# A layer of RWKV attention and mixture of experts: eight settings of its instruction planner, and the issuing engine of the last transfer

## The chip, the cores and the metric

The kernel runs on one core of a Trainium2 chip. Time is device time in microseconds (us), and the number that counts is the median over runs of the kernel: 462.02 us from 3 runs (461.55 to 462.97). The engines are called PE (TensorE, matrix products), PEld (its weight loads), DVE (VectorE), ACT (ScalarE), POOL (GpSimd) and SP (SyncE, which issues most transfers).

## What is computed

The input x has 2 x 2048 tokens of 256 channels in f32. It is normalized, and from the normalized xn two branches are computed and added to x:

```python
x = L0_attn_x                       # (2, 2048, 256)
xn = _layernorm(x, axis=-1)
x = x + attention(xn) + moe(xn)

# attention: v, r = xn @ value_w.T, sigmoid(xn @ recep_w.T)
# a scan over time with the state (aa, bb, pp):
#   wkv_t = (e1 * aa + e2 * v_t) / (e1 * bb + e2 + 1e-6)
#   aa = e1b * aa + e2b * v_t ;  bb = e1b * bb + e2b
# out = (r * wkv) @ out_w.T

# moe: scores = softmax(xn @ gate_w.T + gate_b), the best 2 of 8 experts
# each expert: (silu(xn @ w1.T + b1) * (xn @ w3.T + b3)) @ w2.T + b2
# a shared expert of the same form, hidden size 512, for every token
```

## The kernel before, in words

**Tiles.** The 4096 tokens are 8 chunks of 512. `ORDER` is 2, 3, 0, 1, 4 (called `FIRST`) and 5, 6, 7 (called `LAST`). A time step s of the attention covers the chunks 2s and 2s + 1, one for each batch row.

**Stages.** Each chunk is loaded, normalized, transposed by PE (L579) and copied out of PSUM (L593). Router scores are made (by_e L602, by_t L612, sc L615). When all eight chunks are scored, VectorE does the routing (L651 to L768, with two small counting products on PE, cp L690 and L691): each token is given two slots among 66 tiles of 128 rows. POOL then scatters the normalized rows to those slots in DRAM (xs_d, L795, 64 transfers). The tiles follow in the order `SEQ`: 25 double tiles of 256 rows for one expert (`double_flow`, ph L1357, silu L1343, product L1370, pos L1380, bias L1387), and single or mixed tiles (`tile_flow`, L1255 to L1307). POOL scatters their results to ys_d (L1319). When the last tile is stored, `collect_flow` loads the two results of every token (y, L1400), VectorE adds them with their weights to the chunk's sum (`combine_flow`, L1410), and the chunk goes to the output in halves (`out_flow`, L1446), the very last one in quarters.

Beside this runs the dense work. The shared expert has four pieces of 128 hidden channels for each chunk (`hidden_flow`: p L1003, silu L1009, gated product L1023 on VectorE, or L1016 and L1019 on ACT and POOL for pieces that are planned while the routing runs). The attention has, for each of 4 time steps and 2 halves of the channels, a chain on VectorE and ACT (`attention_flow`, L872 to L921) and for each batch row a flow with the products v and r (`mix_flow`, L935; uu L945, scan L950, rw L957, th L963, L967 to L977). `dense_flow` multiplies hidden pieces and attention with their output weights (po L1086) and adds them to the chunk's sum (L1102; L1112 for the closing quarters). A chunk's sum begins as x plus a bias (L1046). The sums of `FIRST` chunks go to DRAM (part_d) in between and are taken up again; those of `LAST` chunks begin only at the end.

**What sets the order.** Nothing is scheduled at run time: every engine goes through its instructions in the order in which the program lists them. A planner (class `Plan`) writes that list. Each piece of work is a generator, a flow, that asks for an engine and a duration in ns (`on(690, "DVE")`), for rooms (buffers such as the 8 PSUM banks `PS` or the 32 general buffers `U`), and may wait for events. The planner takes the request that can start first by its own durations. Among those that can start within 150 ns of it on the same engine it takes the one with the lowest rank. `plan.add(flow, rank)` gives a flow's rank, and `rank=` in a single request overrides it. `spare=(PS, n)` says that n banks must be left free. Ranks that matter here: routing 0.5, transposes 1.0 to 1.7, collecting 3, tiles 10, the projections v and r 9, the attention chain 20, the mix flows 20 to 23, L1023 15, dense work of `FIRST` 25 to 34, hidden pieces 30 and more, dense sums of `LAST` 45 to 47, combines 45.

**Settings that the change touches:**

- `BETWEEN` (used where the hidden flows are added, at the end of the function): for these chunks of the order the first hidden piece gets the rank of the transposes instead of 30 and more.
- `EAGER`: the attention begins when this chunk of the order is transposed.
- `AHEAD`: hidden pieces of the first `LAST` chunk (chunk 5) that may be made before the tiles and are kept in their U buffers until the end.
- all other pieces of `LAST` chunks wait for the event `turn` of a tile near the end of `SEQ` (its first products have been listed).
- `SOON`: how many tiles ahead `goes_flow` loads the row numbers of a group of eight tiles (meta L1233, then L1237 and L1238), which the scatters to ys_d need.

Of the kernel before, what the change touches and what calls it, by code (L numbers as in the profile page):

```python
# [51 lines left out]
NT = W // P  # L52
# [124 lines left out]
def on(ns, engine, *take, table=None, spare=None, rank=None):  # L177
    return ({engine: ns}, table, take, spare, rank)
# [14 lines left out]
NT = W // P  # L193
# [12 lines left out]
DBL = 2 * (PAIRS // (2 * P) - (E - 1))  # L206
# [6 lines left out]
SEQ = sorted(PLACE, key=PLACE.get)  # L213
assert sorted(SEQ) == [*range(0, DBL, 2), *range(DBL, TILES)]
AT = {j: n for n, j in enumerate(SEQ)}
# [24 lines left out]

LATE = 3000

BETWEEN = (1, 3)

EAGER = 6
MORE = 8

QUICK = 2
# [4 lines left out]

WARM = 10

SOON = 8

BACK = 5

AHEAD = [(LAST[0], i) for i in range(3)]  # L260

LEFT, RIGHT = ORDER[:4], ORDER[4:]

# [2 lines left out]
def rwkv_moe_kernel(  # L266
# [55 lines left out]
    def rows(t, c):  # L322
        return t[c % B, ts(c // B, W), :].rearrange("(n p) c -> p n c", p=P)
# [460 lines left out]
    def scatter_flow():  # L784


        yield have["routed"]
        yield 600
        for side, chunks in (("left", LEFT), ("right", RIGHT)):
            for c in chunks:  # L790
                for n in range(NT):
                    g = c * NT + n
                    for w in range(2):
                        yield on(1410, "POOL")
                        step = nc.gpsimd.indirect_dma_start(  # L795
                            out=xs_views[2 * g + w],
                            out_offset=bass.IndirectOffsetOnAxis(ap=slot[w][:, g : g + 1], axis=0),
                            in_=xn[c][:, n, :],
                            in_offset=None,
                        )  # L800
                        if w:
                            keep_pace(step)
                land(0, [scattered[c]])
            early[side].__exit__(None, None, None)
            if side == "left":
                pool = ctx.enter_context(tc.tile_pool(name="bias", bufs=1, side="left"))
                late["b2"] = pool.tile([P, E, C], F32, tag="b2", name="b2")
                late["still"] = ctx.enter_context(tc.tile_pool(name="still", bufs=3, side="left"))
                late["rows"] = ctx.enter_context(tc.tile_pool(name="late_rows", bufs=2, side="left"))
                late["bcol"] = ctx.enter_context(tc.tile_pool(name="bcol", bufs=3, side="left"))  # L810
                plan.add(bias_flow(), 0)
            else:
                late["pool3"] = ctx.enter_context(tc.tile_pool(name="late3", bufs=2, side="right"))
                late["ys"] = ctx.enter_context(tc.tile_pool(name="late_ys", bufs=3, side="right"))
                late["h"] = ctx.enter_context(tc.tile_pool(name="late_h", bufs=3, side="right"))
        yield LATE
        for j in SEQ:
            plan.add((double_flow if j < DBL else tile_flow)(j), 10 + AT[j] / 100)
        for j in TOGETHER:
            plan.add(rows_flow(j), 10 + AT[j] / 100)  # L820
            flow = still_flow if j < DBL else one_flow if j < UNI else quarters_flow
            plan.add(flow(j), (9 if j < DBL else 15) + AT[j] / 100)
        for j in range(0, TILES, GO):
            plan.add(goes_flow(j), 10 + needed(j) / 100)
        plan.add(collect_flow(), 3)
# [99 lines left out]
    def mix_flow(s, ch, b, e1b, e2b, e1, e2, ready, of_state, of_v, left):  # L925
        c = B * s + b
        of = f"{c}_{ch}"
        yield turned[c]
        yield have["wa"]
        yield ready  # L930

        def project(name):
            pt = bank([P, W], f"{name}p_{of}")
            for k in range(NC):
                nc.tensor.matmul(  # L935
                    pt, wa[name][:, k, ts(ch, P)], xnT[c][k], start=(k == 0), stop=(k == NC - 1)
                )
            xnT_used(c)
            return pt

        yield on(1722, "PE", (PS, 1), spare=(PS, 2), rank=9)
        v = project("wv")
        yield on(690, "DVE", single("uu"))
        uu = wide("uu", of)
        nc.vector.tensor_tensor(uu, e2b, v, ALU.mult)  # L945
        yield on(1400, "DVE", single("aa"))
        aa = wide("aa", of, W + 1)
        state = st_aa[:, b, ch : ch + 1]
        nc.vector.tensor_copy(aa[:, 0:1], state)
        nc.vector.tensor_tensor_scan(aa[:, 1:], e1b, uu, aa[:, 0:1], ALU.mult, ALU.add)  # L950
        nc.vector.tensor_copy(state, aa[:, W:])
        single("uu")[0].give()
        yield of_v
        yield on(690, "DVE", (U, 1))
        wkv = u([P, W], f"rw_{of}")
        rw[c, ch] = wkv
        nc.vector.tensor_tensor(wkv, e2, v, ALU.mult)  # L957
        PS.give()
        yield on(1722, "PE", (PS, 1), spare=(PS, 2), rank=9)
        r = project("wr")  # L960
        yield on(600, "ACT", single("th"), table="tanh" if plan.table not in ("exp", "silu") else plan.table)
        th = wide("th", of)
        nc.scalar.activation(th, r, AF.Tanh, scale=0.5)  # L963
        PS.give()
        yield of_state
        yield on(690, "DVE")
        nc.vector.tensor_tensor(aa[:, :W], aa[:, :W], e1, ALU.mult)  # L967
        left[0] -= 1
        if left[0] == 0:
            for name in ("e1", "e2", "e1b", "e2b"):  # L970
                single(name)[0].give()
        yield on(690, "DVE")
        nc.vector.tensor_tensor(wkv, wkv, aa[:, :W], ALU.add)
        single("aa")[0].give()

        yield on(690, "DVE")
        nc.vector.scalar_tensor_tensor(wkv, th, 1.0, wkv, ALU.add, ALU.mult)  # L977
        single("th")[0].give()
        rw_done[c, ch].set()


    def hidden_flow(c, i):

        if (c, i) not in HALVES:
            yield turned[c]
        yield have["ws13", i]
        if c in LAST and (c, i) not in AHEAD:
            yield turn[SEQ[-8]]
        pts = []
        halves = 2 if (c, i) in HALVES else 1  # L990
        for h in range(halves):
            if halves == 2:
                yield half_turned[h]
            of = ts(h, W // halves)
            for m in range(2):
                yield on(
                    1722 // halves, "PE", *([(PS, 2), (U, 1)] if m == h == 0 else []),
                    spare=(U, KEEP if c in FIRST or (c, i) in AHEAD else MORE),
                )
                if h == 0:  # L1000
                    pts.append(bank([P, W], f"p{m}_{c}_{i}"))
                for k in range(NC):
                    nc.tensor.matmul(  # L1003
                        pts[m][:, of], ws13[:, m, k, ts(i, P)], xnT[c][k][:, of], start=(k == 0), stop=(k == NC - 1)
                    )
        xnT_used(c)
        si = u([P, W], f"si_{c}_{i}")
        yield on(690, "ACT", table="silu")
        nc.scalar.activation(si, pts[0], AF.Silu, bias=vec[:, V_BS1 + i : V_BS1 + i + 1])  # L1009
        PS.give()  # L1010
        bs3 = vec[:, V_BS3 + i : V_BS3 + i + 1]
        if have["scores"].at is not None and have["routed"].at is None:

            yield on(690, "ACT", (U, 1))
            t = u([P, W], f"gate_{c}_{i}")
            nc.scalar.activation(t, pts[1], AF.Identity, bias=bs3)  # L1016
            PS.give()
            yield on(1150, "POOL")
            nc.gpsimd.tensor_tensor(si, si, t, ALU.mult)  # L1019
            U.give()  # L1020
        else:
            yield on(750, "DVE", rank=15)
            nc.vector.scalar_tensor_tensor(si, pts[1], bs3, si, ALU.add, ALU.mult)  # L1023
            PS.give()
        hid[c, i] = si
        hid_done[c, i].set()
# [41 lines left out]
    def dense_flow(c, half, shared, attended, ready, done):  # L1068
# [28 lines left out]
        if closes:  # L1097
            return
        yield ready
        yield on(690, "DVE")  # L1100
        both = sums[c][:, 2 * half : 2 * half + 2, :]
        nc.vector.tensor_tensor(both, po, both, ALU.add)  # L1102
        PS.give()
# [225 lines left out]
    def double_flow(j):  # L1329
# [18 lines left out]
        for m in range(2):  # L1348
# [9 lines left out]
                        p[m][:, i, :], mine[k][:, m, ts(i, P)], xT[:, k, :], start=(k == 0), stop=(k == NC - 1)  # L1358
                    )
            if m == 0:  # L1360
                plan.add(silu_flow(), 10 + AT[j] / 100)
        find(AT[j] + 1)
        U.give()
        XST.give()
# [76 lines left out]
    def out_flow(c, first, n):  # L1441

        of = sums[c]
        groups = slice(first, first + n)
        yield on(500, "SP")
        nc.sync.dma_start(rows(out, c)[:, groups, :], of[:, groups, :])  # L1446
        yield 3000
        left[c] += n
        if left[c] == NT:
            X.give()  # L1450
# [21 lines left out]
    plan.add(route_flow(), 0.5)  # L1472
    plan.add(scatter_flow(), 0.5)
    plan.add(bias_rows_flow(), 2)
    plan.add(attention_flow(), 20)

    def then_attend(c):

# [90 lines left out]
```

## Time and profile before

| what | value |
|---|---|
| median of 3 runs | 462.02 us |
| the profiled execution, its own time | 462.66 us |
| its span | 461.0 us |
| mean granted TensorE clock | 0.999 |
| instructions | 6864 |
| moved by DMA | 84.93 MB, mean 184 GB/s |

The span runs from the first to the last instruction; 1.66 us of that execution's time lie around it. A line of a profile names an engine, a line of the kernel, an operation and its output and input tiles. A wait is written as "who <- whom", with its sum, count and longest case in us.

In broad stages the core spends 0 to 40 us on loading, normalizing and transposing, 40 to 66 on the routing, up to about 157 on the scatter (with dense work on PE), 162 to 400 on the tiles, and the rest on results:

```profile
core 0: us, PE busy (x) PEld busy (x) DVE busy (x) ACT busy (x) POOL busy (x), PEclk, DMA share, GB/s
0.00:40.00 40.00, 38.08 (x281) 25.75 (x282) 30.01 (x118) 26.14 (x53) 19.22 (x70) 1.00 1.01 270
40.00:162.00 122.00, 119.57 (x378) 70.77 (x377) 99.61 (x190) 33.46 (x59) 75.18 (x67) 1.00 0.55 164
162.00:400.00 238.00, 236.11 (x1129) 162.00 (x1128) 185.59 (x349) 140.09 (x274) 98.86 (x89) 1.00 0.59 162
400.00:440.00 40.00, 40.00 (x132) 24.70 (x131) 30.98 (x60) 4.75 (x8) 2.19 (x2) 1.00 0.82 276
440.00:461.00 21.00, 15.92 (x73) 13.37 (x71) 15.44 (x31) 0.00 (x0) 0.00 (x0) 0.97 0.63 213
```

The columns are the stretch and its length, then the busy time and the number of instructions of each engine, the granted clock of TensorE, the DMA engines' share and their rate.

### The profile page before, as it was taken

To read this page: it belongs to the slowest core of one execution; us is meant where nothing else is said; L and a number is where in the kernel's file an instruction comes from. 1 tells how busy PE (TensorE), PEld (TensorE's weight loads), DVE (VectorE), ACT (ScalarE), POOL (GpSimd) and SP (SyncE) were. 2 spreads that over 40 slices of the span, in tenths; PEclk is the share of its full clock that TensorE was granted. 3 is DMA by queue.
4 is the path that set the end of the run, shared out by engine and by line. 5 is a ranking of instruction groups with operands and counts; after the bars stand their busy time and mean duration, and the time that the engine had idled before them with its cause. 6 is when DMAs were issued, how large, how long until landed. Compare 5 with 4: busy or idle time off the path is not lost.

```text
span 461.0 us, 6864 instructions
## 1 busy us (share of the span) xinstructions
PE 449.7 (98%) x1985; PEld 296.6 (64%) x1985; DVE 361.6 (78%) x747; ACT 204.4 (44%) x392; POOL 195.5 (42%) x228
## 2 busy tenths in 40 slices
PE   8999899999999989999999999999999999999996
PEld 6664555444787567766767666666765766646875
DVE  6986999968569658997568966986898568788586
ACT  3788210171140219635873569727662763121000
POOL 5730358777777104355434444362536233300000
PEclk9999999999999999999999999999999999999999
DMA  7999942745234697776584697456656330079993
GB/s 234 352 269 189 238 153 80 228 150 183 92 129 148 206 187 213 188 188 176 131 244 122 181 249 211 124 164 166 188 166 213 113 104 25 25 248 302 345 320 126
DMA packets 91508, 84.93 MB, mean 184 GB/s; under 512 B 50445, under 2 KB 76846, under 8 KB 91344
## 3 DMA queue, kind: packets, MB, share of 16 engines
q1 hardware_dynamic: 82672, 61.98, 47.9%
q0 software_dynamic: 7952, 22.23, 15.3%
q10 hardware_dynamic: 848, 0.30, 0.3%
q8 instruction: 16, 0.26, 0.3%
q14 instruction: 20, 0.16, 0.1%
HBM read 44.93 MB, written 26.70 MB: 155 GB/s over the span
## 4 chain that ended last, share of the span: by engine, by line
PE 75%; DVE 11%; DMA 8%; SPq 2%; ACT 1%; issue 1%; DVEq 0%
PE ph L1357 17%; PE p L1003 16%; PE pos L1380 9%; PE po L1086 8%; PE wrp L935 6%; PE wvp L935 5%; PE ph L1255 4%; PE ph L1259 3%; DMA xb<-in_x_dram 2%; DMA out_dram<-pa 2%; PE pos L1297 2%; PE tp L579 2%; PE pos L1301 1%; DVE xb L1410 1%; DMA xn<-in_x_dram 1%; DMA y<-ys_d 1%
## 5 line engine op out<-in xcount | busy, mean ns | idle before, releaser
L1319 POOL DMA_INDIRECT ys_d<-ys,goes x66 | 75.3, 1140 | 142.3 <-DVE ys L1387 63.6
L1003 PE MATMUL p<-xnT,ws 128*128 128x512 f32 (+1 forms) x272 | 115.3, 569 | 1.5 <-DVE rw L957 1.1
L1357 PE MATMUL ph<-xsT,still 128*128 128x256 f32 x400 | 93.0, 380 | 0.0
L1003 PEld LDWEIGHTS p<-xnT,ws 128*128 128x128 f32 x272 | 50.5, 190 | 53.8 <-issue 47.0
L795 POOL DMA_INDIRECT xs_d<-xn,slot x64 | 71.0, 1110 | 30.7 <-issue 14.9
L1357 PEld LDWEIGHTS ph<-xsT,still 128*128 128x128 f32 x400 | 74.8, 190 | 14.1 <-issue 3.9
L1086 PE MATMUL po<-ws,si 128*128 128x256 f32 x256 | 59.4, 380 | 0.5 <-DVE si L1023 0.5
L1086 PEld LDWEIGHTS po<-ws,si 128*128 128x128 f32 x256 | 48.3, 190 | 10.4 <-issue 2.6
L1009 ACT ACTIVATE si<-p,vec 128x512 f32<-128x512 f32 x32 | 21.6, 686 | 74.3 <-PE p L1003 74.2
L1380 PE MATMUL pos<-we,si 128*128 x200 | 48.4, 385 | 1.4 <-DVE si L1370 1.4
L1380 PEld LDWEIGHTS pos<-we,si 128*128 128x128 f32 x200 | 37.0, 190 | 16.6 <-issue 4.3
L1185 ACT COPY own<-we 128x512 f32 x72 | 38.9, 623 | 1.3 <-issue 1.2
L963 ACT ACTIVATE th<-wrp 128x512 f32<-128x512 f32 x16 | 9.5, 596 | 59.2 <-PE wrp L935 59.1
L1343 ACT ACTIVATE si<-ph,bcol 128x256 f32<-128x256 f32 x50 | 21.0, 471 | 29.4 <-PE ph L1357 29.2
L1086 PE MATMUL po<-wo,rw 128*128 128x256 f32 x128 | 31.9, 379 | 0.0
L1387 DVE TENSOR_TENSOR ys<-pos,b 128x512 f32<-128x512 f32 x25 | 17.2, 690 | 17.2 <-PE pos L1380 16.7
L935 PE MATMUL wrp<-xnT,wr 128*128 128x512 f32 x64 | 30.4, 597 | 0.0
L1370 DVE SCALAR_TENSOR_TENSOR si<-ph,bcol,si 128x256 f32<-128x256 f32 x50 | 21.5, 470 | 9.5 <-PE ph L1357 8.8
L935 PE MATMUL wvp<-xnT,wv 128*128 128x512 f32 x64 | 28.8, 592 | 0.0
L1213 DVE STREAM_TRANSPOSE xsT<-xs 128x512 f32<-128x512 f32 (+1 forms) x41 | 24.0, 594 | 5.8 <-DMA xs<-xs_d 5.8
L1023 DVE SCALAR_TENSOR_TENSOR si<-p,vec,si 128x512 f32<-128x512 f32 x29 | 21.4, 743 | 8.6 <-PE p L1003 7.0
L916 DVE RECIPROCAL bb<-bb 128x128 f32<-128x128 f32 x32 | 27.5, 913 | 0.4 <-issue 0.2
(167 smaller groups left out, 614.2 us busy)
## 6 DMA issues: line engine op xcount, KB each, us to landing
still<-we SPq DMA_DIRECT2D x25, 512.0 KB, 3.2
y<-ys_d SPq DMA_DIRECT2D x32, 256.0 KB, 5.3
xs<-xs_d SPq DMA_DIRECT2D x100, 64.0 KB, 2.9
we<-in_w_exp_dram SPq DMA_DIRECT2D x16, 256.0 KB, 11.3
xb<-in_x_dram SPq DMA_DIRECT2D x8, 512.0 KB
pa<-part_d SPq DMA_DIRECT2D x8, 512.0 KB, 5.5
xn<-in_x_dram SPq DMA_DIRECT2D x14, 256.0 KB, 5.2
part_d<-xb SPq DMA_DIRECT2D x5, 512.0 KB, 2.9
```

The costliest lines, as they stand in the source:

```text
L795: step = nc.gpsimd.indirect_dma_start(out=xs_views[2 * g + w], out_offset=bass.IndirectOffsetOnAxis(ap=slot[w][:, g : g + 1], axis=0), in_ ...
L916: nc.vector.reciprocal(den[:, ts(n, P)], den[:, ts(n, P)])
L935: nc.tensor.matmul(pt, wa[name][:, k, ts(ch, P)], xnT[c][k], start=(k == 0), stop=(k == NC - 1))
L1003: nc.tensor.matmul(pts[m][:, of], ws13[:, m, k, ts(i, P)], xnT[c][k][:, of], start=(k == 0), stop=(k == NC - 1))
L1009: nc.scalar.activation(si, pts[0], AF.Silu, bias=vec[:, V_BS1 + i : V_BS1 + i + 1])
L1086: nc.tensor.matmul(po[:, j, :], l[:, ts(2 * half + j, P)], r, start=(i == 0), stop=(i == len(parts) - 1))
L1185: nc.scalar.copy(mine[q, k], we[:, which[j, q], 0:2, k, :])
L1213: nc.vector.transpose(xT.rearrange("p k (b t) -> p b k t", t=Q), t.rearrange("p b (k i) -> p b k i", i=Q))
L1319: nc.gpsimd.indirect_dma_start(out=ys_views[j], out_offset=bass.IndirectOffsetOnAxis(ap=goes[:, j : j + 1], axis=0), in_=y, in_offset=None ...
L1357: nc.tensor.matmul(p[m][:, i, :], mine[k][:, m, ts(i, P)], xT[:, k, :], start=(k == 0), stop=(k == NC - 1))
L1370: nc.vector.scalar_tensor_tensor(si[:, i, :], p[1][:, i, :], mine["b"][:, 1, i : i + 1], si[:, i, :], ALU.add, ALU.mult)
L1380: nc.tensor.matmul(po[:, t, :], si[:, i, ts(t, P)], we[:, e, 2, i, :], start=(i == 0), stop=(i == NI - 1))
```

## The change

It changes settings of the planner, and in one place the engine that issues a transfer. Nothing that is computed changes.

- `BETWEEN` gains the third chunk of the order; `EAGER` goes from 6 to 5, `SOON` from 8 to 6, `AHEAD` from three pieces to four (all of chunk 5).
- The tiles' rank goes from 10 to 8.5 (their row loads and the doubles' silu with them), the attention chain's from 20 to 12.
- The projections v and r leave one spare PSUM bank instead of two.
- The late hidden pieces wait for the fifth tile from the end instead of the eighth.
- The dense sums of `LAST` chunks get rank 44, where combines have 45.
- The last transfer of the last chunk is issued by ScalarE instead of SyncE.

```diff
-BETWEEN = (1, 3)
+BETWEEN = (1, 2, 3)
-EAGER = 6
+EAGER = 5
-SOON = 8
+SOON = 6
-AHEAD = [(LAST[0], i) for i in range(3)]
+AHEAD = [(LAST[0], i) for i in range(4)]
...
         for j in SEQ:
-            plan.add((double_flow if j < DBL else tile_flow)(j), 10 + AT[j] / 100)
+            plan.add((double_flow if j < DBL else tile_flow)(j), 8.5 + AT[j] / 100)
         for j in TOGETHER:
-            plan.add(rows_flow(j), 10 + AT[j] / 100)
+            plan.add(rows_flow(j), 8.5 + AT[j] / 100)
...
-        yield on(1722, "PE", (PS, 1), spare=(PS, 2), rank=9)
+        yield on(1722, "PE", (PS, 1), spare=(PS, 1), rank=9)
         v = project("wv")
...
-        yield on(1722, "PE", (PS, 1), spare=(PS, 2), rank=9)
+        yield on(1722, "PE", (PS, 1), spare=(PS, 1), rank=9)
         r = project("wr")
...
         if c in LAST and (c, i) not in AHEAD:
-            yield turn[SEQ[-8]]
+            yield turn[SEQ[-5]]
...
         yield ready
-        yield on(690, "DVE")
+        yield on(690, "DVE", rank=44 if c in LAST else None)
         both = sums[c][:, 2 * half : 2 * half + 2, :]
         nc.vector.tensor_tensor(both, po, both, ALU.add)
...
             if m == 0:
-                plan.add(silu_flow(), 10 + AT[j] / 100)
+                plan.add(silu_flow(), 8.5 + AT[j] / 100)
...
-        yield on(500, "SP")
-        nc.sync.dma_start(rows(out, c)[:, groups, :], of[:, groups, :])
+
+        last = (c, first + n) == (DONE[-1], NT)
+        yield on(500, "ACT" if last else "SP")
+        (nc.scalar if last else nc.sync).dma_start(rows(out, c)[:, groups, :], of[:, groups, :])
...
-    plan.add(attention_flow(), 20)
+    plan.add(attention_flow(), 12)
```

## The prediction

> **What bounds the kernel now.** I read the page's engine shares first, then the waits of TensorE, then its timeline around each wait, and last the timeline of the final ten microseconds. The shares:
>
> ```profile
> span 461.0 us, 6864 instructions
> ## 1 busy us (share of the span) xinstructions
> PE 449.7 (98%) x1985; PEld 296.6 (64%) x1985; DVE 361.6 (78%) x747; ACT 204.4 (44%) x392; POOL 195.5 (42%) x228
> ```
>
> TensorE works all the time, and the granted clock is 0.999. The change adds and removes no matmul, so those 449.7 us stay. What can change is the other 11.3 us. The waits of PE, longest first:
>
> ```profile
> engine line waited for: us in total, times, longest us
> PE pos L1380 <- DVE si L1370: 1.4, 2, 1.2
> PE cp L690 <- DVE bb L905: 1.3, 1, 1.3
> PE p L1003 <- DVE rw L957: 1.1, 1, 1.1
> PE warm_ps L450 <- POOL ones L369: 1.1, 1, 1.1
> PE po L1086 <- DVE si L1023: 0.5, 1, 0.5
> PE pos L1301 <- ACT hsT L1287: 0.5, 1, 0.5
> PE p L1003 <- DVE xnT L587: 0.4, 1, 0.4
> PE tp L579 <- DVE xn L556: 0.3, 1, 0.3
> ```
>
> That is 6.6 us: 1.8 at the start (L450, L587, L556) and 4.8 inside. The last matmul ends at 456.5, so 4.5 more lie behind it; 6.6 + 4.5 = 11.1, all but 0.2. If every inner wait went, the gain would be 4.8 us, 1.0%. So small things decide, and they lie in four places: the routing (40 to 66 us), the PSUM shortage behind it (74 to 78), the first expert tiles (162 to 178), and the end:
>
> ```profile
> 447.12 0.70 PE L1086 MATMUL po<-ws,si 128*128 128x256 f32 x2 [0.53 <-DVE si L1023]
> ...
> 448.11 6.50 DVE L1410 SCALAR_TENSOR_TENSOR xb<-y,score,xb 128x256 f32<-128x256 f32 x14
> ...
> 454.53 1.88 DVE L1102 TENSOR_TENSOR xb<-po,xb 128x512 f32<-128x512 f32 x3
> 455.24 2.69 SPq L1446 DMA_DIRECT2D out_dram<-xb  x5
> 455.43 1.03 PE L1086 MATMUL po<-wo,rw 128*128 128x256 f32 x4
> 456.32 0.74 DVE L1112 TENSOR_TENSOR xb<-po,xb 128x256 f32<-128x256 f32 x2
> ```
>
> Columns are start, duration, engine, line. VectorE does fourteen combines in a row, then three dense sums whose products had long been ready, then the two closing sums. SP issues five results back to back.
>
> **The change, part by part.** Every edit but one alters only the order that the planner writes out.
>
> *Last transfer on ScalarE, sums ahead of combines (rank 44 under 45).* The second L1112 ends at 457.06, but its transfer starts at 457.44, because SP's fourth issue (456.90 + 0.49) stands before it: 0.38 us. ScalarE is idle from 439.1 on and nothing is queued behind its new wait. Its issue of a transfer of the same 128 KB cost 0.39 and 0.45 us (the two x loads) against SP's 0.49 here: equal. [...] With the three L1102 (3 x 0.63 us from start to start) done as their products end, the first L1112 no longer starts late and the second starts at 456.46 + 0.1 instead of 456.65: 0.1. SP's burst thins out as well, which is the same 0.38 and not counted twice. Sum: -0.4 to -0.5; bounds 0 and -0.6, and +0.2 if ScalarE's issue costs what its slowest did (0.63). **-0.5.**
>
> *The wait at 446.6.* The gated product L1023 of the last hidden piece started at 446.32, although its matmuls ended at 440.1, because it stood behind a bias sum and combines that waited for transfers. The changed end (fourth piece done earlier, last hidden pieces gated on the fifth tile from the end instead of the eighth, sums placed first) moves that piece. Bounds: -0.53, and +1.9 if it lands behind one transfer wait more (VectorE's longest there was 2.4, of which 0.5 is paid already); I take the end at which it leaves this queue, because that piece's matmuls come earlier by one piece. **-0.5.**
>
> *Fourth kept piece, goes loads two tiles later (SOON 6).* At 165.6 VectorE had idled 3.94 us for a row load, and the first tile's L1370 stood behind it in the queue (silu ready 165.1, start 168.35). PE filled with half a hidden piece (165.81, 1.72 us) and then waited 1.20, and 0.24 more at 178. A fourth piece is 8 matmuls, 8 x 0.43 = 3.44 us of filler in this stretch: more than 1.44. Of nine meta loads (0.47 us each on SP), two move two tiles back; one of them stood among SP's issues of 160 to 164, ahead of row loads: 0.5 us of relief. Coming two tiles later costs the stores nothing: POOL's L1319 waited 116 us for finished tiles (63.6 + 52.5), never for a goes value. Price: the piece holds one U buffer for the whole stage. Bounds: -1.44, 0. **-1.4.**
>
> *Tiles 8.5 instead of 10, so ahead of the projections (9).* In 162 to 400 us PE is idle for 1.9 of 238 us. Both kinds are ready work; swapping them moves 1.72 us blocks. Five 1.72 us blocks of L1003 lie between 348.6 and 397.1; the later gate can push these behind the tiles, so the last tile may end up to 8 us earlier, and the y loads (first at 405.74) with it. PE ends when its work ends, so this gives nothing itself; it widens the slack of the result stage (last combine 454.6, PE 456.5: 1.9 us). Loss: fewer fillers at the end of the tiles, at most one wait of 1.4. **0.**
>
> *Third early piece (BETWEEN).* 3.44 us of PE, one silu (0.69) and one L1023 (0.75) move ahead of the last chunks' transposes. Routing starts at 40.24 after the last by_t; it can come 0 to 3.4 us later, and behind it cp L690, the 64 scatters on POOL (61.8 to 152) and the first tile. PE has the same work meanwhile, and the kept piece covers 3.4. If not, the y loads slip and 1.9 us of slack is spent first. **0.**
>
> *Attention a chunk earlier (EAGER 5) and rank 12.* Its first operation at 32.46 can move up about 1 us (the four copies L593 of two chunks ran from 30.8 to 32.9, and it now waits for the first of the two); the bb scan at 51.78 fills a wait of the routing anyway. The wait of 1.33 at L690 has another source: L662, L665 and L678 took 0.92, 0.96 and 1.57 us where the same shapes took 0.42, beside three GpSimd products L1019 (1.4 us). [...] So the row stays: 0; bounds -1.3, +0.7 for a fourth such piece. **0.**
> Rank 12 against L1023's 15 is the unsafe edit. At 66.1 VectorE now does two L1023 first (1.40), then the attention chain to 73.5 (6.1), pp (1.6) and the mix. Put behind the chain, the two L1023 give back their PSUM banks at 73 to 75 instead of 67. PE wants one for the piece that it starts at 73.28: 0 to 1.8 us. The next wait, 1.10 for L957, has unchanged work before it. Bounds: -1.1 (attention early enough frees v sooner), +1.8. I take the row as it is: **0.** One spare bank instead of two for projections goes with it.
>
> Sum: -0.5 - 0.5 - 1.4 = -2.4. The profiled execution took 462.66 us, 1.66 beside its span; it would come to 460.3. It lies 0.64 above the median of 462.02, so the median goes to 459.6.
>
> **The rivals.**
> *Slower: PSUM banks held behind attention.* The mechanism just named, at each early attention chain. The chains (reciprocals at 68.9, 105.5, 138.8) each take 4 to 7 us of VectorE; if each makes PE wait the full 1.8, that is 5.4, and 462.0 + 5.4 - 2.4 = 465.0. It decides from 3.8 us of such waits on, where gains of 2.4 turn into a loss of 1.4. For it: VectorE is 97% busy from 60 to 82 (21.3 of 22 us), and at 76.9 PE had to wait for the bank that L957 gives back. Against: later it idles (1.58 us at 150.7, 5.13 at 123), and the planner counts banks.
> *A new order, new waits.* Only the end's 0.5 is a saving by construction; all other waits depend on how a static queue meets real DMA times, and others of the same size come in their place: 461.5.
> *More than forecast.* The 1.1 at L957 and the 1.3 at L690 go as well: 459.6 - 2.4 = 457.2. Below that there is little: start, matmuls and drains remain.
>
> **How the numbers follow.** The forecast has 0.38 (459.6; its own range 458.5 to 460.6), the larger gain 0.11, new waits for old 0.26, bank starvation 0.25. A measurement of this kernel tells about 0.3% (1.4 us) from no change: 460.6 to 463.4 is "same". So faster 0.49, same 0.26, slower 0.25. The range leaves out a tenth on each side: 457.4 to 465.0.
>
> **What would show it.** Right: PE's waits inside sum to about 2.9 instead of 4.8; none at the first pos L1380; the last L1102 done before the last combines or right at its product's end; the last out_dram on ACT within 0.1 us of L1112's end; PE busy still 449 to 450. Wrong: PE waits between 66 and 145 on L1023, L957 or L945 above 2 us; y loads beginning after 408 and VectorE ending over 1 us behind PE; a PE busy time that changes.

## The result and the profile after

The changed kernel is slower: 466.85 us, median of 4 runs (466.36 to 467.25), against 461.87 for the kernel before (461.55 to 462.97, 4 runs with those already shown). The ratio is 1.0102, with a 95% interval of 1.0085 to 1.0119. The forecast of 459.6 was wrong in sign, and the time lies above the range. The profiled execution took 466.36 us, 1.66 beside its span.

The page of the changed kernel begins so:

```profile
span 464.7 us, 6842 instructions
...
PE 450.0 (97%) x1985; PEld 297.8 (64%) x1985; DVE 363.2 (78%) x747; ACT 201.4 (43%) x390; POOL 193.1 (42%) x228
```

PE has the same work as before (449.7). PE's waits, inferred from its semaphores:

```profile
PE po L1086 <- DVE si L1023: 5.0, 2, 4.0
...
PE cp L690 <- DVE bb L905: 0.4, 1, 0.4
```

Three of the old inner waits are gone (L1380 1.4, L957 1.1, L1301 0.5) and L690 fell from 1.3 to 0.4. In their place stands one of 4.0, for the gated product L1023. PE's timeline shows where:

```profile
76.87 5.20 PE L1086 MATMUL po<-ws,si 128*128 128x256 f32 x16 [3.98 <-DVE si L1023]
81.91 1.88 PE L935 MATMUL wrp<-xnT,wr 128*128 128x512 f32 x4
83.62 3.62 PE L1086 MATMUL po<-ws,si 128*128 128x256 f32 x16
```

The L1003 before it (from 60.71) end at 72.89, so PE runs out there and goes on at 76.87. Two groups of 16 of the same matmuls follow: the first takes 5.04 us to the next start (76.87 to 81.91), the second 3.46 (83.62 to 87.08). VectorE's timeline of the same stretch shows what it did meanwhile:

```profile
68.32 0.69 DVE L910 TENSOR_TENSOR bb<-e,bb 128x512 f32<-128x512 f32 x1
...
69.84 3.39 DVE L916 RECIPROCAL bb<-bb 128x128 f32<-128x128 f32 x4
...
76.06 2.07 DVE L1023 SCALAR_TENSOR_TENSOR si<-p,vec,si 128x512 f32<-128x512 f32 x3
```

The routing ends at 68.41. Then comes the whole attention chain (rank 12), and only behind it, at 76.06, the three gated products (rank 15), of the hidden pieces (3,2), (3,3) and (0,1). A piece is named by chunk and number. In the kernel before, two of them stood directly behind the routing, and the product L1086 that reads them began at once (VectorE, then PE):

```profile
66.11 1.40 DVE L1023 SCALAR_TENSOR_TENSOR si<-p,vec,si 128x512 f32<-128x512 f32 x2
```

```profile
66.13 7.31 PE L1086 MATMUL po<-ws,si 128*128 128x256 f32 x32
```

Three windows of PE in the changed kernel, with busy time, instructions, granted clock, DMA share and rate:

```profile
73.08:76.49 3.41, 0.00 (x0) 1.00 0.22 78
76.49:79.90 3.41, 3.03 (x7) 0.50 0.26 90
79.90:83.32 3.42, 3.42 (x14) 1.00 0.29 104
```

From 76.5 to 79.9 us, for 3.4 us, the clock is at half: that is the slow first group. At the end of the kernel VectorE's timeline now reads:

```profile
459.77 0.42 DVE L1112 TENSOR_TENSOR xb<-po,xb 128x256 f32<-128x256 f32 x1
460.11 1.00 DVE L1410 SCALAR_TENSOR_TENSOR xb<-y,score,xb 128x256 f32<-128x256 f32 x2
461.21 0.42 DVE L1112 TENSOR_TENSOR xb<-po,xb 128x256 f32<-128x256 f32 x1
```

PE's last matmul ends at 458.07 (before 456.46), but VectorE's last sum ends at 461.63 (before 457.06). The two closing sums now stand behind combines. From that last sum to the end of the span it takes 3.07 us (before 3.94). The result stage, from the first y load to that sum, is longer too: 55.05 us instead of 51.32, with 3.0 us more of VectorE's work in it. The first row is of the kernel before, the second of the changed one; the third engine is VectorE:

```profile
405.74:457.06 51.32, 50.18 (x188) 35.27 (x186) 42.34 (x83) 4.03 (x6) 0.00 (x0) 1.00 0.84 283
406.58:461.63 55.05, 50.45 (x177) 33.17 (x175) 45.33 (x87) 5.41 (x8) 0.00 (x0) 1.00 0.81 274
```

So there are two questions: is the stall at 72.9 with its half clock the loss, and why does VectorE end 3.6 us behind PE? Theory A: the stall and the clock make the loss and pass on to all that follows. Rival B: the order of the end makes it, with sums ahead of combines and results that wait for transfers.

### The profile page after: what moved, and what is told of

The parts are those of the page before. It is cut to its first block, busy times and chain, and to the rows that moved or that the text cites. A ratio compares the mean times of both kernels' runs of the same rounds, so it can differ in the third digit from the quotient of the medians.

```text
span 464.7 us, 6842 instructions
## 1 busy us (share of the span) xinstructions
PE 450.0 (97%) x1985; PEld 297.8 (64%) x1985; DVE 363.2 (78%) x747; ACT 201.4 (43%) x390; POOL 193.1 (42%) x228
## 4 chain that ended last, share of the span: by engine, by line
PE 79%; DVE 11%; DMA 7%; SPq 1%; issue 1%; ACT 0%; DVEq 0%
PE ph L1357 19%; PE p L1003 16%; PE po L1086 11%; PE pos L1380 10%; PE wrp L935 6%; PE wvp L935 5%; PE ph L1255 4%; DMA out_dram<-pa 3%; PE ph L1259 3%; PE pos L1297 2%; DVE xb L1410 2%; PE tp L579 1%; DMA ws<-in_w_sh_dram 1%; PE pos L1301 1%; DMA y<-ys_d 1%; DVE pa L1410 1%
## 5 line engine op out<-in xcount | busy, mean ns | idle before, releaser
L1319 POOL DMA_INDIRECT ys_d<-ys,goes x66 | 70.8, 1072 | 144.7 <-DVE ys L1387 70.8
L1003 PE MATMUL p<-xnT,ws 128*128 128x512 f32 (+1 forms) x272 | 115.4, 569 | 0.6 <-DVE xnT L587 0.4
L1357 PE MATMUL ph<-xsT,still 128*128 128x256 f32 x400 | 92.9, 380 | 0.0
L1357 PEld LDWEIGHTS ph<-xsT,still 128*128 128x128 f32 x400 | 74.9, 190 | 15.6 <-issue 5.2
L1003 PEld LDWEIGHTS p<-xnT,ws 128*128 128x128 f32 x272 | 50.5, 190 | 53.0 <-issue 48.5
L795 POOL DMA_INDIRECT xs_d<-xn,slot x64 | 69.3, 1082 | 27.6 <-issue 16.1
L1086 PE MATMUL po<-ws,si 128*128 128x256 f32 x256 | 61.3, 387 | 5.0 <-DVE si L1023 5.0
L1086 PEld LDWEIGHTS po<-ws,si 128*128 128x128 f32 x256 | 49.5, 194 | 16.5 <-DVE si L1023 6.2
L1380 PE MATMUL pos<-we,si 128*128 x200 | 47.9, 382 | 0.0
L1380 PEld LDWEIGHTS pos<-we,si 128*128 128x128 f32 x200 | 37.5, 190 | 13.3 <-issue 3.8
L1009 ACT ACTIVATE si<-p,vec 128x512 f32<-128x512 f32 x32 | 21.7, 686 | 52.7 <-PE p L1003 52.5
L1086 PE MATMUL po<-wo,rw 128*128 128x256 f32 x128 | 31.9, 379 | 0.0
L935 PE MATMUL wvp<-xnT,wv 128*128 128x512 f32 x64 | 29.8, 595 | 0.0
L1086 PEld LDWEIGHTS po<-wo,rw 128*128 128x128 f32 x128 | 24.2, 190 | 4.1 <-issue 1.0
L1276 ACT ACTIVATE sis<-h 128x256 f32<-128x256 f32 x16 | 6.7, 416 | 45.2 <-DVE h L1270 45.1
```

Of the source, the lines that this page charges most:

```text
L795: step = nc.gpsimd.indirect_dma_start(out=xs_views[2 * g + w], out_offset=bass.IndirectOffsetOnAxis(ap=slot[w][:, g : g + 1], axis=0), in_ ...
L935: nc.tensor.matmul(pt, wa[name][:, k, ts(ch, P)], xnT[c][k], start=(k == 0), stop=(k == NC - 1))
L1003: nc.tensor.matmul(pts[m][:, of], ws13[:, m, k, ts(i, P)], xnT[c][k][:, of], start=(k == 0), stop=(k == NC - 1))
L1086: nc.tensor.matmul(po[:, j, :], l[:, ts(2 * half + j, P)], r, start=(i == 0), stop=(i == len(parts) - 1))
L1319: nc.gpsimd.indirect_dma_start(out=ys_views[j], out_offset=bass.IndirectOffsetOnAxis(ap=goes[:, j : j + 1], axis=0), in_=y, in_offset=None ...
L1357: nc.tensor.matmul(p[m][:, i, :], mine[k][:, m, ts(i, P)], xT[:, k, :], start=(k == 0), stop=(k == NC - 1))
```

## Experiments

The planner's settings cannot be changed one at a time without a new order of all that follows. In most experiments (e1, e2, e5 to e7, e9 to e14), therefore, the order of picks of the changed kernel, which the expectations call after, is written out as a list and played back, with single entries moved. In the others the planner writes a new order. The kernels ran in four sets of four, each with runs of the kernel before. Before took 461.9 us in the first set and 462.35 in the last (both on the chip numbered 9), and 469.3 and 470.8 in the two between (chips 15 and 7, called noisy below, with single runs from 466 to 474). What counts is therefore the ratio to before in the same set. It is estimated over all runs and can differ from the quotient of the medians, by up to 0.002 on the noisy chips.

### e1: two gated products ahead of attention

```diff
 VectorE's list behind the routing
+L1023 si of (3,2)
 L910, L912
+L1023 si of (3,3)
 L916 x4, L918, L921, L872 to L877
-L1023 si of (3,2)
-L1023 si of (3,3)
 L1023 si of (0,1)
```

> After's order, kept as it stands, with one thing moved: two of the three L1023 (gated products of chunk 3's kept pieces) stand ahead of and inside the attention chain of 68 to 76 us instead of behind it. Theory A (the stall at 72.9 makes the loss: 3.98 us of TensorE waiting, and about 1.6 us more because the granted clock then falls to 0.50, and both are passed on to everything behind): about 461.3 (460.5 to 462.5), no wait at L1086 behind the routing, granted clock 1.0 in 60 to 80 us. Rival B (the end's order makes the loss: sums ahead of combines, attention's last operations between them, results that wait for the DMA engines): 464.5 or more, although the wait is gone, since the result stage takes it back.

Measured: 461.8 us (460.48 to 463.51), ratio 0.999 (0.9977 to 1.0002). PE's timeline:

```profile
72.56 3.62 PE L1086 MATMUL po<-ws,si 128*128 128x256 f32 x16
76.01 1.88 PE L935 MATMUL wrp<-xnT,wr 128*128 128x512 f32 x4
```

PE works on from 60.54 to 87 us without a wait, at a clock of 1.00, and the next hidden piece starts at 81.37 instead of 87.08, 5.7 us earlier. By the medians 5.0 us of it reach the end. A holds: moving two instructions of 0.74 us takes back the whole loss, and B's 464.5 did not come. But the kernel is only as fast as before, and the longer result stage is still there (54.86 us). So the two costs add up: the stall turns a small gain into a loss, and without the stall the longer stage keeps that gain near zero; see e6 to e14.

### e2, e5, e9: is it the wait or the clock?

Each puts matmuls by ones into a bank that the next product overwrites anyway, at one place only (its condition is left out below). A trace shows each of these matmuls as two instructions (18 as x36 in e2, 17 as x34 in e9).

```diff
 # e2: into the bank of the waiting product (chunk 3, half 0)
 po = bank([P, 2, C], ...)
+[nc.tensor.matmul(po[:, 0, :P], ones, ones, start=True, stop=True) for _ in range(18)]
 # e5 and e9: into the bank of the last four L1003 ahead of the stall, 36 and 17 of them
 pts.append(bank([P, W], ...))
+[nc.tensor.matmul(pts[m][:, :P], ones, ones, start=True, stop=True) for _ in range(17)]
```

> After's order with 18 matmuls of 128x128 by ones put ahead of the waiting product L1086 of chunk 3, half 0: TensorE has something to do for about 1.5 us of the 4.0 us wait, whose end stays where it is (the bank is overwritten behind it, so the result is the same). Tells apart wait and clock inside theory A. If the fall of the granted clock costs 1.6 us by itself: about 465.2 (464.7 to 466), clock near 1.0 in 76 to 81 us. If the clock is of no account, or the end is set elsewhere (B): 466.8.

Measured: 472.82 us (471.83 to 473.26), ratio 1.0219 (1.0176 to 1.0262), worse than either theory had it. The filler itself waited:

```profile
77.28 6.89 PE L1084 MATMUL po<-ones 128*128 128x128 f32 x36 [3.97 <-DVE si L1023]
```

In that profile the product L1086 starts only at 84.01, behind all of the filler. The expectation was built wrongly, and the miss tells something. These matmuls read only ones. That they wait for L1023 all the same means that the bank was not free: it is one that L1023 gives back. So the stall is a wait for a PSUM bank as well as for the gated piece that the product reads a few matmuls later. A single move of L1023 cures both, and neither was tried alone. By an estimate the read alone would have cost most of it, 3.1 us: with a free bank the first four of the product's 16 matmuls (0.9 of 3.46 us), which read pieces gated earlier, could have run, and then PE would have waited all the same.

> After's order with 36 matmuls of 128x128 by ones put into the bank of the last four L1003 ahead of the stall (they are overwritten by the next start). That bank is free when they come, unlike the one that the first filler of this kind was put into, so TensorE works from 71 to 77 us and waits for nothing; the product of chunk 3 starts when the gated piece is ready, as in after. What is left of the loss is the time without work, what is gone is only the fall of the clock. If that fall costs 1.6 us by itself: 465.2 (464.5 to 465.8), granted clock 1.0 from 70 to 82. If it costs nothing: 466.8 or more (the 36 matmuls take up to 4 us and may come out 0.3 too long).

Measured: ratio 1.0027 (1.0005 to 1.0049). The filler was twice too long (72 instructions of 0.114 us), but PE was never idle, the clock stayed at 1.00, and the product took 3.45 us from its start to the next (80.81 to 84.26) instead of 5.04. The ratio is lower than expected, although the product came 3.9 us later than in the changed kernel; why is not known. On that chip such a difference is not read: e6 and e7, whose lists differ only in their last 15 us, began their y loads there at 410.30 and 406.99.

> As the kernel with 36 filling matmuls, but with 17: the profile of that one showed them as 72 instructions of 0.114 us, 8.2 us in all, so that chunk 3's product started at 80.8 instead of 76.9. 17 x 2 x 0.114 = 3.9 us just fill the stall of 72.9 to 76.9. The wait stays in time, only as work; gone is the fall of the clock. In that profile the product took 3.45 us from its start to the next, in after 5.04, so: after less 1.6, a ratio to before of 1.0067 (1.004 to 1.009; 465.0 on a chip where before takes 461.9), granted clock 1.0 from 70 to 84. If the clock is not what made the 1.6: 1.010.

Measured: ratio 1.0059 (1.0032 to 1.0087), against an expected 1.0067 and 1.0102 for the change; on a noisy chip this match counts for little. What is read is PE's timeline:

```profile
70.82 3.96 PE L1001 MATMUL p<-ones 128*128 128x128 f32 x34
...
76.66 3.72 PE L1086 MATMUL po<-ws,si 128*128 128x256 f32 x16 [0.17 <-DVE si L1023]
80.22 1.88 PE L935 MATMUL wrp<-xnT,wr 128*128 128x512 f32 x4
```

The product starts when it did in the changed kernel (76.66 against 76.87), but is through in 3.56 us. So 1.5 to 1.6 us of the stall's price are clock, and 4.0 are wait.

### e16: the attention rank alone, on the kernel before

```diff
-    plan.add(attention_flow(), 20)
+    plan.add(attention_flow(), 12)
```

> The kernel before with the attention rank 12 instead of 20 and nothing else; the planner writes a new order with it, whose own end is 2.8 us later than that of before. If attention ahead of the gated products is a loss by itself: 1.006 (1.003 to 1.012), with a wait for L1023 behind the routing. If it costs only together with the third early piece and the new dense order: 1.000.

Measured: 466.88 us, ratio 1.0094 (1.0063 to 1.0125). PE's timeline, and then VectorE's:

```profile
74.41 9.33 PE L1086 MATMUL po<-ws,si 128*128 128x256 f32 x32 [4.95 <-DVE si L1023]
83.58 1.88 PE L1003 MATMUL p<-xnT,ws 128*128 128x512 f32 x4
```

```profile
73.61 2.07 DVE L1023 SCALAR_TENSOR_TENSOR si<-p,vec,si 128x512 f32<-128x512 f32 x3
```

This one number, with the new order that the planner writes for it, gives the same picture: the chain first (from 65.87), L1023 7.7 us later, a wait of 4.95, and 9.17 us for 32 matmuls that took 7.15 before (66.13 to 73.28). Of the nine settings that changed, this one alone costs about as much as all of them together. (The profile is of e16's fastest run, 465.27 us.)

### e3, e4, e8, e15: the end's edits one by one

```diff
 # e3: the change without rank 44
-        yield on(690, "DVE", rank=44 if c in LAST else None)
+        yield on(690, "DVE")
 # e4: the change with its last transfer on SP;  e8, e15: the kernel before with its last transfer on ACT
```

> After with the dense sums L1102 of the last chunks at their former rank (behind the combines); the stall at 72.9 stays. Theory A: 466 to 467, the order at the end is worth at most 0.8. Rival B: about 463.8 (463 to 465), as the combines then no longer stand behind sums and the last results go out earlier.

Measured: 466.12 us (465.21 to 467.56), ratio 1.0084 (1.0061 to 1.0107): the change's own time within the intervals, and not B's 463.8.

> After with its last transfer issued by SP again, nothing else. Both theories: slower by what the issue from ScalarE saves; by the tails of the two profiles (3.07 us from the last L1112 to the span's end against 3.94) 0.9 us, so 467.3 to 467.8; by the issue times alone (0.38 us late on SP before) 467.2. If SP stands free when the last L1112 ends, 466.9: then the step is worth nothing in this order.

Measured: 466.76 us, ratio 1.0091 (1.0064 to 1.0118): nothing, which was the third of the written cases.

> The kernel before with its last transfer issued by ScalarE and nothing else. The prediction's step: 0.38 us less, 461.5, since SP's fifth issue stood behind its fourth. By the tails (3.94 us behind the last L1112 in before, 3.07 after): 0.9 less, 461.0. If it is worth nothing here either, as in after: 461.9.

Measured: ratio 1.0015 (0.9988 to 1.0041), on a noisy chip.

> The kernel before with its last transfer issued by ScalarE, once more: on the noisy chip 1.0015 (0.9988 to 1.0041). The prediction's step: -0.38 us, 0.9992. By the tails: -0.9, 0.998. Nothing: 1.000.

Measured: 462.6 us, ratio 1.0001 (0.998 to 1.0021). The profile shows more than the ratio. VectorE's last sum ends at 458.43. SP's last results and ScalarE's issue (two answers of the timeline, one engine each):

```profile
456.60 2.10 SPq L1447 DMA_DIRECT2D out_dram<-xb  x4
```

```profile
458.46 0.37 ACTq L1447 DMA_DIRECT2D out_dram<-xb  x1
```

ScalarE issues 0.03 us after the last sum, where SP had come 0.38 us late. Yet the span (462.3) ends 3.87 us after that sum, as late as before (3.94). The tails of the others: the change 3.07, with SP instead of ScalarE 2.98, without rank 44 but with ScalarE 3.83. So the shorter tail does not come from the issuing engine. It goes with the spacing of the last results: 3.8 to 3.9 us where the last issue starts 0.2 to 0.5 us behind the one before it, 3.0 to 3.1 where rank 44 spreads them (1.4 us). In e16, which has neither rank 44 nor the issue by ScalarE, a late matmul leaves 0.96 us between them, and the tail is 3.16. Rank 44 pays for its shorter tail elsewhere: three pairs of kernels with and without it (1.0102 and 1.0084, e6 and e7, e11 and e12) show no difference that a measurement can tell.

### e6, e10, e7: where did TensorE's 2.8 us go?

Without the stall (e1) PE ends at 453.63, 2.83 us before the old end, and the first y load comes at 402.56 instead of 405.74. VectorE's last sum ends at 457.42, against 457.06 before. The result stage takes 54.9 us instead of 51.3. Its windows in e1, with VectorE's busy time and instructions, PE's clock, DMA share and rate:

```profile
412.56:417.56 5.00, 4.86 (x11) 1.00 0.73 223
417.56:422.56 5.00, 4.37 (x10) 1.00 0.98 322
...
442.56:447.56 5.00, 4.39 (x9) 1.00 0.72 236
```

There are two gaps in the transfers, 10 and 40 us into the stage (0.73 and 0.72; before has 0.99 and 0.96 there). In the first VectorE is full; attention's last operations for chunk 7 (L967, L973, L977) stand between the first combines.

```diff
 VectorE's list in the result stage
 L1410 x2
-L967, L973, L977 of chunk 7
 L1410 x4
 ... (12 us)
 L1023 si of (7,2)
+L967, L973, L977 of chunk 7
 # e7: besides, no rank 44 (new order of the last 15 us)
```

> The kernel that gates chunk 3's pieces ahead of attention, and besides the last chunk's three attention operations L967, L973, L977 are taken from between the first combines (there at 409.65 to 411.8 us) to behind the gated product of piece (7,2), 12 us later. TensorE ended 2.8 us earlier than before in that kernel, y loads began 3.2 us earlier, and still it took as long as before: if those three, 2.1 us of VectorE ahead of a result that the next loads wait for, are what gives the gain back: 459.5 (458.8 to 460.3). If the result stage is bound by its 16 DMA engines or by the three buffers that x, part and result share: 461.0 to 462.0.

> The same, with the dense sums of the last chunks back behind the combines (without rank 44). If rank 44 costs VectorE's combines their start (sums of 0.7 us each ahead of the last ten combines): 0.7 less than with it, 458.8. If the sums are as cheap in front as behind: the same as with it within 0.5; by the prediction's step (three sums out of the way of the two closing ones, 0.1 us): 0.1 slower.

> The kernel with both moves (gated pieces ahead of attention, the last three attention operations behind the combines) once more, on another chip: on the chip of its first run before itself took 469.3 with runs from 466 to 472, too wide to tell. Its profile there showed that the three operations' place was taken by a wait of 1.65 us of L1023 for TensorE's next piece, so the gain is 0.4 instead of 2.1: ratio to before 0.998 (0.997 to 0.999), 461.0 to 461.5 where before takes 461.9. If the three operations were what held the stage: 0.995.

Measured: e6 0.9974 (0.9938 to 1.0009), e7 0.9976 (0.9946 to 1.0007), and e6 again as e10: 1.0005 (0.9977 to 1.0033), on two noisy chips. No gain over e1 can be told. VectorE's timeline in e6:

```profile
420.95 0.75 DVE L1023 SCALAR_TENSOR_TENSOR si<-p,vec,si 128x512 f32<-128x512 f32 x1 [1.65 <-PE p L1003]
421.62 2.83 DVE L1410 SCALAR_TENSOR_TENSOR pa<-y,score,pa 128x256 f32<-128x256 f32 x6
```

The place of the three became a wait: the next combines stand behind an L1023, and that waits for PE's piece. So e6 did not free the combines, and its ratios lie nearer to the rival's 461 to 462 us (transfers and buffers) than to 459.5; the two are not told apart by it.

### e11 to e14: closing the two gaps

```diff
 # e11: e6, and L1023 of (6,3), (7,0), (7,1) two to three combines later in VectorE's list
 # e12: e11 without rank 44
 # e13: e11, and e14: e1, each with one entry moved in SP's list
+out_dram<-pa  second half of chunk 4
 xb<-in_x_dram of chunk 6    (waits for a buffer)
 y<-ys_d
-out_dram<-pa  second half of chunk 4
```

> The same, and three of the L1023 in the result stage (pieces (6,3), (7,0), (7,1)) stand two to three combines later in VectorE's queue, so that no combine waits behind an L1023 for TensorE's piece. If that queue is what eats the 2.8 us that TensorE is early: y loads and results follow each other sooner and the end comes 1.0 to 2.0 us earlier, ratio 0.995 (0.993 to 0.997). If the stage is bound by its transfers (DMA share 0.95 and more in most of it, three buffers for part, x and result): as the kernel without this move, 0.998.

> The same without rank 44 (sums of the last chunks behind the combines). On the noisy chip with and without it came out within 0.4 us of each other. If the sums ahead of the last ten combines cost the end what they take (2 x 0.6 us between the last x load and the last combines): 0.5 to 1.2 us less than with it. By the prediction's step: 0.1 us more.

Measured: 0.9983 (0.9958 to 1.0008) and 0.9998 (0.9968 to 1.0028). The first gap was closed (share 1.00 and 0.99 in 5 to 15 us of the stage), the second stayed (0.62 at 35 to 40 us). No gain over e10 can be told, and e11's 0.998 is again the rival's figure. This is what remains in SP's queue in e1, shown with e14, where one entry is moved:

```profile
435.95 0.38 SPq L1033 DMA_DIRECT2D xb<-in_x_dram  x1
...
436.98 0.39 SPq L1448 DMA_DIRECT2D out_dram<-pa  x1
...
442.69 0.38 SPq L1033 DMA_DIRECT2D xb<-in_x_dram  x1
```

```profile
434.58 0.41 SPq L1448 DMA_DIRECT2D out_dram<-pa  x1
...
440.14 0.38 SPq L1033 DMA_DIRECT2D xb<-in_x_dram  x1
```

The result at 436.98 was ready since 433.7, but stood behind an x load that waited for a buffer; and it is the transfer whose landing frees the buffer of the last x load (442.69). One move brings that load 2.55 us forward.

> The kernel with gated pieces ahead of attention, attention's last operations and three L1023 of the result stage behind combines, and now besides one result moved in SP's queue: the second out of chunk 4 goes ahead of the x load of chunk 6, which waits for a buffer, instead of behind it. In the profile without this move the result's combines ended at 433.7 and its issue came at 437.0, and the last x load waited until 442.7 for that buffer. Theory: the gap 40 us into the stage goes, the last x load comes 2 to 3 us earlier, and with it the end: ratio to before 0.993 (0.990 to 0.996). Rival: transfers fill the 16 DMA engines and the stage stays as long as it is: 0.998.

> The kernel with the gated pieces ahead of attention and nothing else, and the one result moved ahead of the x load in SP's queue. If the second gap alone gives TensorE's 2.8 us back: 0.994 (0.992 to 0.996), the last x load at about 440 instead of 442.7. If both gaps count: 0.997. If neither: 0.999 as without the move.

Measured: e13 460.39 us (459.27 to 461.89), ratio 0.9955 (0.9936 to 0.9973); e14 461.26 us, 0.9977 (0.9958 to 0.9996). Both are faster than before, and e13's interval lies below that of e1 and does not hold the rival's 0.998. So the order of these queues is part of what the stage costs; e14 came out at the figure of "both count", but its interval overlaps those of e1 and e13. The gaps are not gone in e13, they have moved (0.83 and 0.55 in the same windows); what came earlier is the last x load, at 438.07. e14's profile shows how the 2.55 us shrink: VectorE works without a pause from 441.62 to 456.97. The last chunk's bias sum (L1046) starts at 445.86 instead of 446.29 behind what VectorE still has to do for chunk 6, which got its own x load no earlier. Why the stage is still 54.3 us long (51.3 before) is not settled. e13 is the best of all the kernels that ran: 0.45% below before.

## Why the prediction was wrong

| | first y load | PE's last matmul ends | last L1112 ends | result stage | span |
|---|---|---|---|---|---|
| before | 405.74 | 456.46 | 457.06 | 51.3 | 461.0 |
| the change | 406.58 | 458.07 | 461.63 | 55.1 | 464.7 |
| e1 | 402.56 | 453.63 | 457.42 | 54.9 | 460.4 |
| e13 | 402.57 | 453.78 | 456.93 | 54.4 | 460.0 |
| e16 | 408.26 | 459.99 | 460.44 | 52.2 | 463.6 |

Against before, the change begins its y loads 0.84 us later, takes 3.73 longer for the stage and ends 0.87 sooner behind it: 3.7 us. Without the stall (e1) the same sum is -3.18 + 3.54 - 0.96 = -0.6.

**The step that failed: "Rank 12 against L1023's 15 is the unsafe edit ... I take the row as it is: 0", with bounds of -1.1 and +1.8.** The place and the cause were named: the L1023 behind the chain give back their banks at 73 to 75 instead of 67. The price was read at the wrong customer. The prediction asked who wants a bank next and found a piece at 73.28. It did not ask who reads the gated pieces. In the trace of before, 32 matmuls of the product L1086 run from 66.13, right at the end of the routing, and they read the pieces that L1023 gates at 66.11; the trace shows PE's weight load waiting 0.36 us for exactly that. Put the chain in front, and this product has to wait; by then it also wants a bank that L1023 gives back (e2). So PE waits for what is left of 7.7 us when its other work runs out: 4.95 us in e16, 3.98 in the change, whose order gives PE 28 instead of 24 matmuls of L1003 to do first. With the fall of the clock this cost 5.6 us in the change, where the sum has 0 and the bound is 1.8. An upper bound must take the first reader as well as the next user of the buffer.

**A wait was priced at its own length.** The clock fell behind the stall, and the product lost 1.6 us more (e9), in e16 2.0. The prediction had no such term; no wait inside before is longer than 1.33 us, and the clock of before is 1.00 from 5.8 to 459.7 us. The longest single wait in the prediction was 1.8 us, and what one of that length costs in clock no run shows: the missing term follows from the wait that was sized too small.

**The rival was the right story.** "PSUM banks held behind attention", 465.0, chance 0.25, named this mechanism. It spread the price over three chains at 1.8 each. In fact one chain cost 5.6 and the later ones little: in e1 the only such wait, at 107.6, is 0.67. Its point of decision (3.8 us of such waits) was passed by the first stall. What spoke for it, VectorE 97% busy from 60 to 82 us, should have weighed more than "the planner counts banks". The planner counts them by its own durations: the routing ends 4 us later on the chip than in its plan (68.4 against 64.2; before 66.1 against 62.2), and its plan for the change leaves PE without work there already (69.7 to 72.8).

**The fourth kept piece, -1.4: right in the number.** L1380's two waits are gone in the change and in e1. They are gone in e16 as well, which has no fourth piece and another order, so that the piece took them away is not shown.

**The waits at L957 and L690, 0 with bounds of -1.1 and -1.3: the good end.** L957's is gone, in e16 too, so rank 12 is enough for that. L690's fell by 0.9. The prediction had its source right, the operations slowed beside GpSimd's L1019, and was wrong to leave the row as it was: the third L1019 moved from 48.83 to 53.70, away from L678, which took 1.57 us before and 0.62 in the change (in this order):

```profile
49.19 1.57 DVE L678 TENSOR_TENSOR both<-one,one 128x256 f32<-128x256 f32 x1
```

```profile
51.58 0.62 DVE L678 TENSOR_TENSOR both<-one,one 128x256 f32<-128x256 f32 x1
```

The bound of +0.7 for a fourth product on GpSimd is shown by no run: L1019 runs three times before and three times in the change. In e1 PE's inner waits sum to 1.7 us instead of 4.8, and PE ends 2.83 us earlier. On PE alone the prediction was too careful.

**The wait at 446.6, -0.5: wrong.** It is 1.03 in the change and 0.6 in e1; the last L1023 now stands at 447.93 behind a bias sum that waited 2.53 us for a transfer, the end of the bounds that was not taken.

**Last transfer and rank 44, -0.5: wrong in its parts.** ScalarE's issue comes at once, as forecast, and gives nothing (e15, e4). The bound of -0.6 is shown by no run: in e15 the span ends 3.87 us behind the last sum, before 3.94. The thinning of the burst, which the prediction counted as the same 0.38, is the part that works (0.8 to 0.9 us of tail). VectorE then ends later by its combines, and the sum is nil (e3, e7, e12).

**The second failure: tiles ahead of projections, 0, "it widens the slack of the result stage".** The y loads do come 3.2 us earlier in e1, but no slack was won, since the stage is longer by 3.5. Work that before lay ahead of it now lies in it: VectorE is busy 45.25 us there instead of 42.34. Its combines stand between L1023, attention and sums in one list, and its x loads behind buffers; moving seven entries gave back 0.5 of the 3.5 (e13), and the rest is open. Rank 12 alone does not shift it (41.39 us in e16), and without rank 44 it is shifted all the same (45.18 in e3); which of the other edits did it was not tried. Of the gain on PE, e1 hands on 0.5 us (0.999, not distinct from nothing), e13 2.1.

The signs that the prediction named held: a wait on L1023 between 66 and 145 above 2 us (3.98) and VectorE more than 1 us behind PE (3.56). The y loads did not begin after 408, so that sign held by half. But four of the five signs of being right came true as well: no wait at the first pos L1380, the last L1102 at 457.02 ahead of the last combines, ScalarE's issue 0.04 us behind the last L1112, and PE busy for 450.0. Only PE's inner waits, 5.4 us instead of 2.9, spoke against the forecast.

## What to carry to other kernels

When an edit puts a long chain ahead of short operations in a static queue, find for each displaced operation its first reader and the work that covers it until then, and take the cover's end as the price; then do the same for the buffer it frees. Add the clock to a stall of TensorE: those of 4.0 to 5.0 us cost 1.5 to 2.7 us more here than their own length. A gain on the busiest engine counts only as far as the last stage can pass it on, so follow it through that stage's transfers and queues before it is booked.

## What the runs showed of the hardware

**The granted clock fell to 0.50 at the stall behind the routing, and stayed there for 3.4 or 6.8 us.** In the changed kernel it was at half from 76.49 to 79.90 us (the three windows in the section on the result), in e4 from 77.2 to 80.6, in e2 from 76.0 to 82.8 and in e16 from 72.0 to 78.8. In e3, behind the same wait of 4.0 us as in the change, it fell so (columns as there):

```profile
71.80:75.22 3.42, 0.90 (x3) 1.00 0.25 87
75.22:78.63 3.41, 1.96 (x5) 0.50 0.29 102
78.63:82.04 3.41, 3.41 (x10) 0.50 0.23 82
82.04:85.46 3.42, 3.42 (x14) 1.00 0.32 116
```

In e9, where matmuls by ones fill that time, it stays at 1.00 from 72 to 85 us. So waits of the same length cost differently: the product behind 3.97 to 3.98 us took 5.04 us in the change, 5.25 in e4 and 6.19 in e3, against 3.45 at a clock of 1.00 (e5). Nor does the length of a wait alone tell its price in two shorter cases: behind one of 2.15 us in e10 16 matmuls of L1003 took 8.83 us, against 7.03 in before, and behind one of 2.35 in e11 twelve took 5.42, against 5.31 in before; the mean clocks of these two executions are 0.994 and 0.999. What decides when the clock falls, and for how long, was not settled.

**Chips differ by more than the change does.** The kernel before took 461.9 and 462.35 us in two sets on one chip, 469.3 and 470.8 on two others, with single runs spread over 3.9 and 4.8 us on the first and over 5.5 and 6.8 on the others. On those two PE shows waits between 100 and 165 us that the profiles of the first lack (in e8 it waits 1.25 us for a late silu L1009 and 3.5 for gated products, in e7 2.9 for a load of weights, behind which 16 matmuls of L1357 take 5.27 us, against 3.62 in before). What causes them is open.
